# TensorE turns rows in place of DMA transposes, and a search over list schedules orders the attention

## Chip, core and metric

The kernel runs on one core of a Trainium2 chip. The metric is the device time of one execution in microseconds, smaller is better. Engines are named as in the profile: PE is TensorE (PEld its weight loads), DVE is VectorE, ACT is ScalarE, POOL is GpSimd, SP is SyncE, whose only work here is to issue DMAs.

## What is computed

One transformer block with adaptive layer norm, all in float32. `x` is 2 x 2048 rows of 256 features (4096 rows in all).

```
mod = silu(c) @ Wmod                       # six rows of 256 for each of the 2 batches
h   = layernorm(x) * (1 + ca) + sa
x   = x + ga * attention(h)                # 2 heads of 128, one shared k and v, rotary, causal
h   = layernorm(x) * (1 + cb) + sb
gate = softmax(h @ Wg + bg);  thr = sigmoid(h @ Wt + bt) / 8
w    = max(gate - thr, 0), normalised over the 8 experts
x   = x + gb * sum_e w[e] * (gelu(h @ W1[e] + b1[e]) @ W2[e] + b2[e])     # 256 -> 1024 -> 256
```

A row goes only to experts where its weight is above zero, so each expert has a list of rows.

## The kernel before

**Attention stage.** The 4096 rows are 32 tiles of 128. For each tile the function `tile_steps` declares small steps: load `x` (L505), moments (L476 to L483), normalise (`xn`, L516), transpose on PE (`pt`, L525), scale and shift (`hT`, L533/L535), project (`pq`, L548/L553), rotate, scores (`psc`, L600, with a mask matmul L604), exponent (L627), transpose of the probabilities (`ptr`, L673) and their copy out (L677), the product with v (`pav`, L683), the output projection (`po`, L717), residual (L724), second norm (`hx`, L740/L743), the row store to `feats` (L759) and the gate logits (`pl`, L787). For 28 of the 32 tiles the transpose of `hx` that the logits need goes by DMA: POOL splits the float32 words into two planes of 16 bits (`hp`, L750), SP stores them to `feats` and issues a DMA transpose (L771), and POOL or DVE joins the halves (L775). The last four tiles transpose `hx` on PE (`ph`, L767) and ACT copies it out (L782).

**What sets the order.** Every step is put into a `Plan` with an engine, an estimated cost, the steps that it follows, the buffers that it takes and gives back (`room`) and a rank. `Plan.run` plays the steps through once: at each time the ready step of lowest rank goes to a free engine. The order found is the order of the instructions on each engine, for good; on the chip semaphores do the waiting. `first` is the rank of what the start needs, ranks of 999 and above belong to the end.

**Between the stages.** While the attention ends, two items of expert 0 are already worked (`pha`, L1055; `pya`, L1072), their rows gathered and transposed by `fetch`, which also prepares the first item of the expert stage (`xT`). Both halves of a `pya` result share one PSUM tile. `hold` loads the row counts of the experts into registers, all eight in one step on PE.

**Expert stage.** Each expert's list is worked in items of 256 rows (`TI`), the last of an expert in 128 if that is enough. Four loops run side by side, coupled by semaphores:

- PE (`item`, L1266): waits for `ready`, does the first product into PSUM `h` (L1272, 8 chunks `f`, over `HB` = 6 rotating banks), then the second into `y` (L1282).
- ACT: gelu from `h` to `g` (L1307).
- POOL: copies an item's row numbers (`at`, L1441), gathers the rows from `feats` into `xr` (two indirect DMAs, L1397), writes part of the next expert's list (L1413 to L1421, four indirect DMAs, in the first items of an expert), and adds the result of an earlier item to `out` (L1431).
- SP (`turn`, L1231): waits for the gather (`loaded`), transposes `xr` to `xp` by DMA (L1239) and raises `planed`.
- DVE: joins the halves into `xT` (L1335) when the first product of the current item is done, then gates and biases (L1350, L1363, L1374).

POOL may gather into `xr` again when `planed` says that it was read.

Of the kernel before, what the change touches and what calls it, by code (L numbers as in the profile page):

```python
# [15 lines left out]
U16 = mybir.dt.uint16  # L16
# [5 lines left out]
P = 128  # L22
# [19 lines left out]
HB = 6  # L42
# [3 lines left out]
class Plan:  # L46
# [19 lines left out]
    def run(self):  # L66
# [10 lines left out]
        while open_ or ends:  # L77
            for n in sorted(open_, key=lambda n: (self.steps[n][6], n)):
                engs, costs, do, _, take, give, _, late = self.steps[n]
                idle = [(e, c) for e, c in zip(engs, costs) if free.get(e, 0.0) <= now]  # L80
                if not idle or ready[n] > now:
                    continue
                eng, cost = idle[0]
                if any(self.room[r] < take.count(r) for r in take):
                    continue
                for r in take:
                    self.room[r] -= 1
                free[eng] = now + cost
                ends.append((now + cost + late, n))
                open_.discard(n)  # L90
                order.append((n, eng))
            times = [e for e, _ in ends] + [f for f in free.values() if f > now]
            times += [ready[n] for n in open_ if ready[n] > now]
            now = min(t for t in times if t > now)
            for e, n in [x for x in ends if x[0] <= now]:
                ends.remove((e, n))
                for r in self.steps[n][5]:
                    self.room[r] += 1
                for m in then[n]:
                    need[m] -= 1  # L100
                    ready[m] = max(ready[m], e + LINK)
                    if need[m] == 0:
                        open_.add(m)
        assert len(order) == len(self.steps)
# [6 lines left out]
def adaln_block_kernel(ctx, tc, x, wqkvT, woT, wgt, bgt, w1, b1T, w2, b2, cT, wmod, rope, out):  # L111

# [37 lines left out]
    b2_bc = const.tile([P, E, D], F32, name="b2_bc")  # L152
    gb_bc = const.tile([P, B, D], F32, name="gb_bc")
    lists = [dram.tile([NTOK, ENT], F32, name=f"list_{e}") for e in range(E)]
    feats = dram.tile([NTOK, 2 * D], U16, name="feats")
# [11 lines left out]
    with tc.manual_schedule():  # L167
        attention(
            tc, x, wqkvT, woT, wgt, bgt, w1, b1T, w2, b2, cT, wmod, rope, out, ident, counts,
            b1_sb, b2_bc, gb_bc, lists, feats, place, entry, weights, wpool,  # L170
# [6 lines left out]
    for e in range(RES, E):  # L177
# [3 lines left out]
    xr = ep.tile([P, CI * 2 * D], U16, name="xr")  # L181
    xp = ep.tile([P, CI * 2 * KD, P], U16, name="xp")
# [10 lines left out]
    mcur = ep.tile([P, CI, ENT], F32, name="mcur")  # L193
    to = ep.tile([P, NW], I32, name="to")
    new = ep.tile([P, NW, ENT], F32, name="new")
    hs = [pp.tile([P, TI], F32, name=f"h{z}") for z in range(HB)]
    ys = [pp.tile([P, D], F32, name=f"y{c}") for c in range(CI)]
    experts(
        tc, nc, lists, feats, out.rearrange("b t d -> (b t) d"), counts, ident, b1_sb, b2_bc,
        gb_bc, w1, w2, weights, xr, xp, kept, gs, gate, part, yb, yo_end, who_end, sheets, at, mcur, to, new,  # L200
# [4 lines left out]
def attention(  # L205
    tc, x, wqkvT, woT, wgt, bgt, w1, b1T, w2, b2, cT, wmod, rope, out, ident, counts,
    b1_sb, b2_bc, gb_bc, lists, feats, place, entry, weights, wpool,
# [6 lines left out]
    room = {"ps": 6, "pav": 2, "x": 9, "s": 16, "pT": 3, "hx": 4, "hp": 3, "qT": 3, "big": 3, "xn": 3,  # L214
            "hT": 2, "hT2": 2, "hpT": 2, "aT": 2, "g_sb": 1, "sign": 1, "size": 1}
# [86 lines left out]
    def load(dst, src, kb, rank=first, **how):  # L302
        return plan.add(
            "SP", max(0.5, kb / 360.0), lambda: nc.sync.dma_start(dst, src), late=2.0, rank=rank,
            **how
# [8 lines left out]
    plan.add("PE", 3.4, lambda: idle_work(8), take=["ps"], give=["ps"], rank=first - 5)  # L314
# [13 lines left out]
    for t0, t1 in [(0, 1), (1, 4)] + [(q, q + 4) for q in range(4, NT, 4)]:  # L328
# [14 lines left out]
    l_b2 = load(  # L343
        b2_bc.rearrange("p e d -> p (e d)"), b2.rearrange("e d -> (e d)").partition_broadcast(P),
        1024, rank=6.0,
    )
# [27 lines left out]

    def by_feature():
        box["pm"] = pm = ps_tile("pm")
        for j in range(2 * KD):
            for k in range(KD):
                nc.tensor.matmul(
                    pm[:, j * B : (j + 1) * B], wm_0[:, k, ts(j, P)], sc[:, k, :],  # L380
                    start=(k == 0), stop=(k == KD - 1),
                )
# [9 lines left out]
    m_pe = plan.add("PE", 2.0, by_feature, after=[s_sc, l_m0], take=["ps"], rank=first)  # L392
# [95 lines left out]
    def tile_steps(b, i, r, group, g):  # L488
# [14 lines left out]
        def load_x():  # L503
# [6 lines left out]
            "SP", 0.5, load_x, late=2.0, take=["x"], rank=first + early[r] if r in early else r  # L510
# [237 lines left out]
        def halves():  # L748
            st["hp"] = work([P, 2, D], "hp", u, U16)
            nc.gpsimd.tensor_copy(  # L750
                st["hp"], st["hx"].bitcast(U16).rearrange("p (d two) -> p two d", two=2)
            )


        by_dma = r < NTOK // P - 4
        n_f = add("POOL", 0.65, halves, [n_h], take=["hp"], give=["hx"] if by_dma else [])
        n_hp = add(
            "SP", 0.5,
            lambda: nc.sync.dma_start(  # L759
                feats[ts(b * NT + i, P), :], st["hp"].rearrange("p two d -> p (two d)")  # L760
            ), [n_f], late=2.0, give=[] if by_dma else ["hp"],
        )
# [6 lines left out]
        def turn_halves():  # L769
            st["hpT"] = work([P, 2 * KD, P], "hpT", u, U16)  # L770
            nc.sync.dma_start_transpose(st["hpT"], st["hp"].rearrange("p two d -> p (two d)"))  # L771

        def join_halves(eng):
            st["hT2"] = work([P, KD, P], "hT2", u)
            of[eng].tensor_copy(  # L775
                st["hT2"].bitcast(U16).rearrange("p k (t two) -> p k t two", two=2),
                st["hpT"].rearrange("p (two k) t -> p k t two", two=2),
            )

        def hT2_out():  # L780
            st["hT2"] = work([P, KD, P], "hT2", u)
            nc.scalar.copy(st["hT2"].rearrange("p k t -> p (k t)"), st["ph"][:, :D])  # L782
# [14 lines left out]
        if by_dma:  # L797
            n_t = add("SP", 1.3, turn_halves, [n_f, n_hp], late=2.2, take=["hpT"], give=["hp"])
            n_t = add(
                ["POOL", "DVE"], [0.66, 0.58], join_halves, [n_t], take=["hT2"], give=["hpT"]  # L800
            )
        else:
            n_t = add("PE", 0.32, turn_h, [n_h], take=["ps"])
            n_t = add("ACT", 0.38, hT2_out, [n_t, n_f], take=["hT2"], give=["ps", "hx"])
# [171 lines left out]
    def fetch(index, u, after, to, take=(), low=low):  # L976
# [3 lines left out]
        def gather():  # L980
            st["xr"] = work([P, CI * 2 * D], "g_sb", "_r" + u, U16)
            for c in range(CI):
                nc.gpsimd.indirect_dma_start(
                    out=st["xr"][:, ts(c, 2 * D)],
# [5 lines left out]
        def turn():  # L990
            st["xp"] = work([P, CI * 2 * KD, P], "sign", "_p" + u, U16)
            nc.sync.dma_start_transpose(st["xp"], st["xr"])

        def join():
            dst = to().bitcast(U16).rearrange("p k (c t two) -> p c k t two", c=CI, two=2)
            src = st["xp"].rearrange("p (c two k) t -> p c k t two", c=CI, two=2)
            for c in range(CI):
                nc.vector.tensor_copy(dst[:, c], src[:, c])

        n = low("POOL", 2.6, gather, after, late=3.0, take=["g_sb"])  # L1000
        n = low("SP", 0.1, turn, [n], late=3.5, take=["sign"], give=["g_sb"])
        return low("DVE", 0.8, join, [n], take=take, give=["sign"])
# [23 lines left out]
    before_gelu = list(last_exp)  # L1026
    for k in range(AHEAD):
# [40 lines left out]
        def second(c, f0, st=st, k=k):  # L1068
            if (c, f0) == (0, 0):
                st["py"] = ps_tile(f"pya_{k}")  # L1070
            for f in range(f0, f0 + NF // 2):
                nc.tensor.matmul(  # L1072
                    st["py"][:, ts(c, D)], st["g", f // 2 * 2][:, ds(f % 2 * TI + c * P, P)], weights[0][1][:, f, :],
                    start=(f == 0), stop=(f == NF - 1),
                )

        def result(c, k=k, st=st):
            yo = kept.yo[k][:, c, :]
            nc.vector.tensor_tensor(yo, st["py"][:, ts(c, D)], b2_bc[:, 0, :], ALU.add)
# [3 lines left out]
        for f0 in range(0, NF, 2):  # L1083
# [5 lines left out]
            )  # L1089
            n_a.append(low(  # L1090
# [4 lines left out]
        for c in range(CI):  # L1095
            for f0 in (0, NF // 2):
# [3 lines left out]
                    take=["ps"] if (c, f0) == (0, 0) else [],  # L1100
                    give=["s"] * (NF // 2) if (c, f0) == (CI - 1, NF // 2) else [],
                )
            n_r.append(low(
                "DVE", 0.85, lambda c=c, result=result: result(c), [n, n_g, l_b2],
                give=["ps", "size"] if c == CI - 1 else [],
# [29 lines left out]
    def hold(name, eng, columns):  # L1135
        def load():
            kept.count[name] = {at: register(nc, eng, counts, at) for at in columns}
# [4 lines left out]
    low("PE", 2.0, hold("PE", nc.tensor, range(E)), [n_total] + n_ahead)  # L1142
# [20 lines left out]
def experts(  # L1163
    tc, nc, lists, feats, rows, counts, ident, b1_sb, b2_bc, gb_bc, w1, w2, weights, xr, xp, kept,
# [49 lines left out]
    with tc.tile_critical():  # L1214
        names = (
            "read", "loaded", "planed", "ready", "first", "act", "second", "taken", "parted",
            "gated", "copied", "named", "biased", "added", "waited", "paused", "indexed", "staged",
# [4 lines left out]
        with nc.Block() as block:  # L1222

            @block.sync
            def _(sync):
# [7 lines left out]
                def turn(t):  # L1233

                    sync.wait_ge(sem["loaded"], t * (16 * CI))
                    sync.sem_inc(sem["paused"], 1)
                    sync.wait_ge(sem["ready"], t + 1)
                    sync.sem_inc(sem["paused"], 1)
                    sync.dma_start_transpose(xp, xr).then_inc(sem["planed"], 16)  # L1239

                sync.sem_inc(sem["planed"], 16)
                done, t0 = 1, 0
                for e in range(E):
                    many = items_of(sync, count(sync, e))
                    if e == E - 1:
                        run(sync, many, NTOK // TI, lambda i: turn(t0 + i))
                    else:
                        a = count(sync, E + e)
                        run(sync, a, NP, lambda i: turn(t0 + done + i))
                        read(e + 1)  # L1250
                        t1 = sync.snap(
# [328 lines left out]
```

## Time and profile before

| | us |
|---|---|
| median of 3 runs (1622.19 to 1622.57) | 1622.2 |
| the profiled execution: its time | 1622.67 |
| the profiled execution: first to last instruction (the span) | 1620.5 |
| PE busy | 1596.6 |
| POOL busy | 907.2 |
| DVE busy | 665.1 |
| ACT busy | 588.2 |
| first product of the expert stage starts | 464.22 |
| last product of the expert stage starts its stretch | 1606.01 |

The mean granted clock of PE is 0.995. A float32 matmul shows as two records in the profile, a transpose on PE as one. The length of a record is its time from start to end in a pipeline, so records overlap; the time that one costs PE is the distance from its start to the start of the next.

### The profile page before, as it was taken

The page shows a single profiled execution, that of the slowest core. Times are in us where ns is not written, and L with a number is a line of the kernel's source. Part 1 is how long each engine was busy: PE and PEld are TensorE (multiplying, and loading weights), DVE is VectorE, ACT ScalarE, POOL GpSimd, SP SyncE. Part 2 cuts the span into 40 slices and gives each one's busy share as a digit, 9 for nine tenths or more (in the row PEclk, how much of TensorE's full clock was granted, in tenths as well). Part 3 has the DMA queues.
Part 4 walks back from the last instruction along what each step waited for, and adds up shares of the span by engine and source line. Part 5 has one row for each costly group of instructions (what it writes and reads, how often), then busy time and mean ns, then how long its engine had stood idle before and what let it go on. Part 6 is the DMA issues. An engine that isn't in the chain of part 4 may idle for free.

```text
span 1620.5 us, 26414 instructions
## 1 busy us (share of the span) xinstructions
PE 1596.6 (99%) x7916; PEld 1361.7 (84%) x7916; DVE 665.1 (41%) x2141; ACT 588.2 (36%) x1385; POOL 907.2 (56%) x1063
## 2 busy tenths in 40 slices
PE   8999999999999999999999999999999999999997
PEld 6877777777878888888888888888888888888886
DVE  6888767567422332323323222222322232222322
ACT  5576665655522222222222222222222222222322
POOL 5656524222147767757757765664776477534433
PEclk9999999999999999999999999999999999999998
DMA  6511111101033353434345334433533333333333
GB/s 237 155 40 50 40 40 30 30 21 43 20 96 59 67 114 59 67 56 111 57 69 111 59 64 92 78 59 59 110 58 66 60 60 60 62 58 58 62 56 48
DMA packets 181521, 111.10 MB, mean 69 GB/s; under 512 B 126354, under 2 KB 172050, under 8 KB 181332
## 3 DMA queue, kind: packets, MB, share of 16 engines
q0 software_dynamic: 41968, 46.83, 18.0%
q1 hardware_dynamic: 131348, 50.43, 13.6%
q10 hardware_dynamic: 8144, 13.11, 2.4%
q8 instruction: 28, 0.46, 0.1%
q14 instruction: 33, 0.27, 0.1%
HBM read 51.44 MB, written 31.87 MB: 51 GB/s over the span
## 4 chain that ended last, share of the span: by engine, by line
PE 95%; issue 1%; DVE 1%; POOL 1%; ACT 1%; another core or an unknown queue 0%; DMA 0%; SPq 0%; POOLq 0%; DVEq 0%; ACTq 0%
PE h L1272 35%; PE y L1282 34%; PE pav L683 7%; PE psc L600 7%; PE ptr L673 3%; PE pq L548 2%; PE po L717 2%; PE pya L1072 1%; PE pha L1055 1%; PE pq L553 1%; PE pl L787 1%; POOL list L900 0%; PE pt L525 0%; DMA x<-in_x 0%
## 5 line engine op out<-in xcount | busy, mean ns | idle before, releaser
L1307 ACT ACTIVATE g<-h,b_sb 128x256 f32<-128x256 f32 (+1 forms) x688 | 317.5, 465 | 838.5 <-PE h L1272 737.1
L1282 PE MATMUL y<-w,g 128*128 128x256 f32 x2640 | 585.8, 379 | 2.3 <-ACT g L1307 1.9
L1272 PE MATMUL h<-xT,w 128*128 128x256 f32 (+1 forms) x2752 | 584.9, 371 | 0.1
L1272 PEld LDWEIGHTS h<-xT,w 128*128 128x128 f32 x2752 | 506.1, 190 | 66.4 <-DVE xT L1335 0.8
L1282 PEld LDWEIGHTS y<-w,g 128*128 128x128 f32 x2640 | 500.4, 190 | 72.8 <-ACT g L1307 4.2
L1431 POOL DMA_INDIRECT out<-yo,who x172 | 277.0, 1610 | 219.3 <-DVE yo L1374 163.2
L1421 POOL DMA_INDIRECT list<-new,to x216 | 221.7, 1027 | 93.6 <-issue 69.1
L1363 DVE TENSOR_TENSOR yb<-y,b_bc 128x256 f32<-128x256 f32 x165 | 62.7, 420 | 422.7 <-PE y L1282 375.3
L1397 POOL DMA_INDIRECT xr<-feats,at x172 | 171.7, 998 | 100.4 <-POOL at L1441 70.3
L1335 DVE COPY xT<-xp 128x512 uint16<-128x512 uint16 x172 | 68.7, 441 | 315.6 <-PE h L1272 156.6
L600 PE MATMUL psc<-kT,qT 128*128 128x512 f32 (+3 forms) x320 | 144.1, 532 | 0.8 <-DVE thr L853 0.8
L683 PE MATMUL pav<-pT,v 128*128 128x256 f32 x544 | 143.7, 386 | 0.3 <-ACT pT L677 0.3
L683 PEld LDWEIGHTS pav<-pT,v 128*128 128x128 f32 x544 | 96.4, 190 | 38.9 <-issue 21.2
L627 ACT ACTIVATE s<-s,nmx 128x512 f32<-128x512 f32 (+3 forms) x160 | 104.5, 656 | 38.5 <-DVE nmx L618 38.3
L611 DVE TENSOR_SCALAR_CACHE_REDUCE s<-psc 128x512 f32<-128x512 f32 (+3 forms) x160 | 96.8, 608 | 50.8 <-PE psc L600 36.1
L677 ACT COPY pT<-ptr 128x512 f32<-128x512 f32 (+1 forms) x144 | 77.6, 562 | 56.6 <-PE ptr L673 50.2
L900 POOL DMA_INDIRECT list<-entry,place x40 | 41.9, 1048 | 80.9 <-DVE place L897 47.1
L1350 DVE SCALAR_TENSOR_TENSOR gate<-gb_bc,mcur,part 128x256 f32<-128x256 f32 x172 | 77.0, 488 | 3.0
L673 PEld LDWEIGHTS ptr<-ident,s 128*128 128x128 f32 x544 | 64.8, 141 | 15.4 <-issue 5.7
L673 PE MATMUL ptr<-ident,s 128*128 128x128 f32 x544 | 77.1, 273 | 0.0
L1441 POOL COPY at<-sheet 128x2 int32 x85 | 61.7, 725 | 13.3 <-DMA xp<-xr 11.1
L1374 DVE TENSOR_TENSOR yo<-yb,gate 128x512 f32<-128x512 f32 (+1 forms) x85 | 57.2, 673 | 3.9
(171 smaller groups left out, 1076.4 us busy)
## 6 DMA issues: line engine op xcount, KB each, us to landing
w<-in_w ACTq DMA_DIRECT2D x12, 1024.0 KB
x<-in_x SPq DMA_DIRECT2D x32, 128.0 KB, 4.3
w<-in_w SPq DMA_DIRECT2D x4, 1024.0 KB
out<-x SPq DMA_DIRECT2D x32, 128.0 KB, 1.7
feats<-hp SPq DMA_DIRECT2D x32, 128.0 KB, 1.7
list<-new,to POOLq DMA_INDIRECT x216
xr<-feats,at POOLq DMA_INDIRECT x172
out<-yo,who POOLq DMA_INDIRECT x172
```

What stands on the lines that cost most here:

```text
L600: nc.tensor.matmul(ps[:, :w], st["qT"][:, h, :], kT[:, ds(c * SC, w)], start=True, stop=not last)
L611: nc.vector.tensor_scalar(s[:, :w], st["sc", h, c][:, :w], scale, None, ALU.mult, ALU.max, accum_out=st["mx", h][:, c : c + 1],)
L627: nc.scalar.activation(s[:, :w], s[:, :w], AF.Exp, bias=st["nmx", h], accum_out=st["den"][:, h, c : c + 1],)
L673: nc.tensor.transpose(ptr[:, j, h, :], s[:, ds((c0 + j) * P % SC, P)], ident)
L677: nc.scalar.copy(pT[:, :m], st["ptr", c0][:, :m])
L683: nc.tensor.matmul(st["pav"][:, : NH * P], v[:, c0 + j, :], st["pT", c0][:, j].rearrange("p h t -> p (h t)"), start=(c0 + j == 0), stop=(c ...
L1272: last = pe.matmul(hs[f % HB][:, :w], weights[e][0][:, k, ts(f, P)], xT[:, k, :w], start=(k == 0), stop=(k == KD - 1),)
L1282: last = pe.matmul(ys[c], gs[f][:, ts(c, P)], weights[e][1][:, f, :], start=(f == 0), stop=(f == NF - 1),)
L1307: act.activation(gs[f][:, :w], hs[f % HB][:, :w], AF.Gelu_apprx_tanh, bias=b1_sb[:, at : at + 1],).then_inc(sem["act"], 1)
L1397: pool.indirect_dma_start(out=xr[:, ts(c, 2 * D)], out_offset=None, in_=feats, in_offset=bass.IndirectOffsetOnAxis(ap=at[:, c : c + 1], ax ...
L1421: pool.indirect_dma_start(out=lists[e], out_offset=bass.IndirectOffsetOnAxis(ap=to[:, j : j + 1], axis=0), in_=new[:, j, :], in_offset=Non ...
L1431: pool.indirect_dma_start(out=rows, out_offset=bass.IndirectOffsetOnAxis(ap=who[:, c : c + 1], axis=0), in_=yo[:, c, :], in_offset=None, c ...
```

## The change

1. **Expert stage.** `xr` holds float32 rows. PE transposes them itself: after the first product of item t it waits for the gather of item t+1 and does four transposes of 128 x 128 into a PSUM tile `xt`, then goes on with the second product. DVE copies `xt` to `xT` in one instruction. SP keeps only the reads of the lists. `xt` takes a PSUM bank, so `HB` goes from 6 to 5. POOL waits for `turned` where it waited for `planed`.
2. **Attention.** All 32 tiles transpose `hx` on PE; ACT or DVE copies it out. The split, the DMA transpose and the join are gone, and `feats` gets `hx` as it is. The gathers of `fetch` (two items ahead and the next) are transposed on PE too.
3. **The order.** `Plan.run` tries 13 schedules with fixed pseudo-random numbers: one with the ranks as written, and twelve in which each kind of step (told by the line of its function) gets a common shift of up to 0.3, 1.0 or 2.0 ranks, for ranks from 1 to 900. The shortest by its own estimate is emitted. Early loads are estimated to land after 3.5 us in place of 2.0, and `room` for `x` is 12 in place of 9.
4. **Start.** The modulation of the first norm (`by_feature`) is made as two matmuls of 512 columns, an ACT copy and four small transposes in place of eight narrow matmuls; the idle matmuls ahead of it are 12 in place of 8, and 3 more follow.
5. **Ends of the attention.** The two halves of `pya` get a PSUM tile each. The eight PE register loads become eight steps among the last products. Four idle matmuls at the start of the expert stage become three.
6. **b2.** Expert 0's row is loaded early (128 KB broadcast in place of 1024 KB); the other seven are loaded by ACT's queue when expert 1 begins.

```diff
-HB = 6
+HB = 5
+TRIALS = (0.0,) + (0.3, 1.0, 2.0) * 4
...
+    def run(self):
+        draw = random.Random(0)
+        kinds = sorted({s[2].__code__.co_firstlineno for s in self.steps})
+        best = (float("inf"), None)
+        for w in TRIALS:
+            by = {k: draw.uniform(-w, w) for k in kinds}
+            best = min(best, self.trial([
+                by[s[2].__code__.co_firstlineno] if 1.0 <= s[6] < 900.0 else 0.0
+                for s in self.steps
+            ]), key=lambda found: found[0])
+        now, order = best
...
-    plan.add("PE", 3.4, lambda: idle_work(8), take=["ps"], give=["ps"], rank=first - 5)
+    plan.add("PE", 5.0, lambda: idle_work(12), take=["ps"], give=["ps"], rank=first - 5)
...
-        if by_dma:
-            n_t = add("SP", 1.3, turn_halves, [n_f, n_hp], late=2.2, take=["hpT"], give=["hp"])
-            n_t = add(
-                ["POOL", "DVE"], [0.66, 0.58], join_halves, [n_t], take=["hT2"], give=["hpT"]
-            )
-        else:
-            n_t = add("PE", 0.32, turn_h, [n_h], take=["ps"])
-            n_t = add("ACT", 0.38, hT2_out, [n_t, n_f], take=["hT2"], give=["ps", "hx"])
+        n_t = add("PE", 0.24, turn_h, [n_h], take=["ps"])
+        add(
+            "SP", 0.5, lambda: nc.sync.dma_start(
+                feats[ts(b * NT + i, P), :], st["hx"].bitcast(I32)
+            ), [n_t], late=2.0, give=["hx"],
+        )
+        n_t = add(["ACT", "DVE"], [0.38, 0.42], hT2_out, [n_t], take=["hT2"], give=["ps"])
...
-        n = low("SP", 0.1, turn, [n], late=3.5, take=["sign"], give=["g_sb"])
-        return low("DVE", 0.8, join, [n], take=take, give=["sign"])
+        n = low("PE", 0.46, turn, [n], take=["ps"], give=["g_sb"])
+        return low("DVE", 0.7, lambda: nc.vector.tensor_copy(to(), st["xt"]), [n], take=take,
+                   give=["ps"])
...
-    low("PE", 2.0, hold("PE", nc.tensor, range(E)), [n_total] + n_ahead)
+    for e, n in enumerate(products[-E - 1 : -1]):
+        plan.add("PE", 0.05, hold("PE", nc.tensor, [e]), after=[n_total, n], rank=999.0)
...
             @block.tensor
             def _(pe):
+                def turn(t):
+                    pe.wait_ge(sem["loaded"], t * (16 * CI))
+                    for c in range(CI):
+                        for k in range(KD):
+                            last = pe.transpose(xt[:, k, ts(c, P)], xr[:, c, ts(k, P)], ident)
+                    last.then_inc(sem["turned"], 1)
+
                 def item(e, i, t, parts):
...
                         last.then_inc(sem["first"], 1)
+                    turn(t + 1)
                     for f in range(NF):
...
                 def ready(t):
-                    dve.wait_ge(sem["planed"], t * 16 + 16)
-                    dst = xT.bitcast(U16).rearrange(
-                        "p k (c t two) -> p c k t two", c=CI, two=2
-                    )
-                    src = xp.rearrange("p (c two k) t -> p c k t two", c=CI, two=2)
-                    for c in range(CI):
-                        last = dve.tensor_copy(dst[:, c], src[:, c])
-                    last.then_inc(sem["ready"], 1)
+                    dve.wait_ge(sem["turned"], t + 1)
+                    dve.tensor_copy(xT, xt).then_inc(sem["ready"], 1)
```

## Prediction

> **What bounds the kernel now.** I read the page first: shares of busy time, clock, the costliest groups.
>
> ```profile
> PE 1596.6 (99%) x7916; PEld 1361.7 (84%) x7916; DVE 665.1 (41%) x2141; ACT 588.2 (36%) x1385; POOL 907.2 (56%) x1063
> ...
> PEclk9999999999999999999999999999999999999998
> ...
> L1282 PE MATMUL y<-w,g 128*128 128x256 f32 x2640 | 585.8, 379 | 2.3 <-ACT g L1307 1.9
> L1272 PE MATMUL h<-xT,w 128*128 128x256 f32 (+1 forms) x2752 | 584.9, 371 | 0.1
> ```
>
> PE is busy 99% at full clock, and ahead of 5392 expert records it idled 2.4 us. A busy PE could still hide bubbles, so next comes the chain of waits in order of time, where a half item of the expert stage is one piece:
>
> ```profile
> 485.52 6.91 PE y L1282 x32
> 492.43 6.91 PE h L1272 x32
> 499.33 6.91 PE y L1282 x32
> ```
>
> 32 records in 6.91 us are 0.216 each, back to back, item after item: 13.82 us an item, and nothing but PE work in it. The list of waits agrees: DVE waits 120.4 us for the DMA transposes, yet all PE waiting on another engine comes to these few lines:
>
> ```profile
> DVE xT L1335 <- DMA xp<-xr: 120.4, 34, 4.2
> ...
> PE pt L525 <- DVE xn L516: 4.3, 3, 2.2
> ...
> PE y L1282 <- ACT g L1307: 1.9, 2, 1.1
> ```
>
> So the DMA transposes are wholly hidden, and work put on PE lengthens the end one for one, unless it falls into one of PE's holes. These are at the start (first projection at 10.80 us), after 30.07 us, and between the stages.
>
> **The price of one transpose on PE.** The trace has 544 like it (`ptr`, float32, 128 x 128). Columns: start, length, line.
>
> ```profile
> 302.47 1.08 PE L683 MATMUL pav<-pT,v 128*128 128x256 f32 x4
> 303.39 1.04 PE L673 MATMUL ptr<-ident,s 128*128 128x128 f32 x8
> 304.26 1.02 PE L600 MATMUL psc<-kT,qT 128*128 128x512 f32 x2
> ...
> 310.12 0.60 PE L673 MATMUL ptr<-ident,s 128*128 128x128 f32 x4
> 310.55 1.03 PE L717 MATMUL po<-woG,aT 128*128 128x256 f32 x4
> ```
>
> Start to start, eight cost 0.87 us and four cost 0.43: 0.109 each. The four `pav` ahead of the eight took 0.92, where four at 0.216 are 0.86, so a switch can add 0.06. The row of one `ptr` gives a mean of 273 ns, but that is its length in the pipeline. The Trainium skill (TensorE: Matmul & The Clock Gate, Part 4: PE-mode transpose) gives about 275 ns in a kernel, and adds that transposes don't engage the full clock. By that rule the change would cost 412 x 0.275 = 113 us; by the start distances, with the clock at 9 in these slices, 45. I take the distances. The skill also calls the DMA path the slow one (VectorE: DVE Perf Modes, The three transpose paths: 1309 ns against 390, for bf16). SP's 86 issues here have a median of 1.24 us, and a sum by that rule would gain some 0.9 us per transpose; the waits above say that nothing on PE waits for them, so I credit 0.
>
> **The change part by part**, against the profiled execution (time 1622.67, span 1620.5, 2.2 around it, 0.5 above the median).
>
> *Expert turns.* L1272 has 2752 records, 32 an item: 86 items, so 86 turns. Four transposes are 0.437, with both switches up to 0.51; I take 0.47: 86 x 0.47 = +40.4 (37.6 to 43.8). Nothing hides it. Queued behind `turn` on PE is the second product, and behind that everything. The copy to `xT` (two join copies of 0.43 before, one PSUM read now, like the 0.42 of L1363 per 256 columns, so about 0.8) has the 6.9 us of the second product to hide in. `HB` 5 costs nothing: chunk 5 starts 4.3 us into an item, and the gelu that frees its bank ended 1.6 us in (464.22 to 465.86); without that cover each item would pay the difference. In two places, mid-`y`, PE waits for the gelus of a 128-row item; the turn gives ACT 0.47 us there: -0.9.
>
> *The new wait on the gather.* The gather must now land by the end of the first product; before, it had until some 4 us ahead of the item's end, for transpose and join. First item of the stage:
>
> ```profile
> 464.22 7.07 PE L1272 MATMUL h<-xT,w 128*128 128x256 f32 x32
> ...
> 468.56 0.19 POOL L1441 COPY at<-sheet 128x2 int32 x1
> ...
> 469.59 1.02 POOL L1397 DMA_INDIRECT xr<-feats,at  x1 [0.83 <-POOL at L1441]
> ...
> 470.91 0.95 POOL L1397 DMA_INDIRECT xr<-feats,at  x1 [0.30 <-issue]
> ...
> 471.13 7.07 PE L1282 MATMUL y<-w,g 128*128 128x256 f32 x32
> ...
> 473.99 15.44 SPq L1239 DMA_TRANSPOSE xp<-xr  x2
> ```
>
> SP issues at 473.99, so the gather landed about then, 2.8 us after the first product ended at 471.13: PE stands still, +2.8 (0 to 4), with the second product queued behind. Second item: POOL's next gather was taken up by SP at about 488.2 (473.99 + 15.44 - 1.24). The new PE comes to its second turn at 474.0 + 0.5 + 6.9 + 6.9 = 488.3: just in time. From there POOL's period with list writing is 13.5 (`at` at 482.33, 495.82, 509.26), while PE's is 13.82 + 0.47 = 14.29, so the slack grows by 0.8 an item: 0 further. POOL's own wait, `turned`, is raised half an item before it comes round again; its list writes and adds queue behind it, and DVE's `who` waits for the adds.
>
> *Attention transposes.* 28 tiles x 2, and 3 x 4 for the fetched items: 68 x 0.109 = +7.4. The second price (ACT 0.37 or DVE 0.42 per copy) replaces 0.68 on POOL for the join or 0.45 on DVE, and POOL loses 32 splits of 0.68; POOL and SP get lighter, DVE (up to 43 of 50 us busy) and ACT (up to 32 of 50) hardly change. SP has 31 fewer transpose issues and the row store waits for `hx` alone. Behind `turn_h` on PE lie scores and products of other tiles, with ACT's copies waiting on them; the order puts it where `hx` is estimated done, and estimates of the same quality leave PE nearly without waits today: 0.
>
> *Start.* PE was cold until 14.4 us (the clock in windows of 1 us: 0.50 from 8 to 14). More idle work may keep it warm: projections spaced 0.213 at 10.80 and 0.109 later, so up to -1.7. Against it, `modT` gets longer: 0.65 on ACT, 0.4 on PE and two handovers, while the first idle stretch (3.46 for 16 records) grows by half. I take -1 (-3 to +2).
>
> *Order and buffers.* The hole of 2.2 us after 30.07 waits for an `xn` whose chain lies behind the modulation rows on DVE; it may go or move: -1 (-2 to +2). More `x` buffers and the 1024 KB of b2 off the early queue help only there. Elsewhere the middle of the attention has little to give: `thr` at 138 us cost 0.8.
>
> *Between the stages.*
>
> ```profile
> 457.12 1.99 PE L1072 MATMUL pya<-w,s_g 128*128 128x256 f32 x8 [0.52 <-DVE yo L1079]
> 460.56 1.35 PE L312 MATMUL pi<-ident 128*128 128x128 f32 x10 [1.45 <-issue]
> 463.26 1.13 PE L1294 MATMUL y<-ident 128*128 128x128 f32 x8 [1.34 <-issue]
> ```
>
> Eight records from 457.12 end at 458.85. The 1.7 us until 460.56 I read as the eight register loads, moved under queued products now; the 0.52 wait for `yo` goes with the second PSUM tile; one idle matmul less is 0.2. Together -2.4. If a register load finds `counts` not yet written, PE stops and this turns to +2. The b2 load of expert 1 has a whole item to land before DVE needs it: 0.
>
> Sum: 40.4 - 0.9 + 2.8 + 7.4 - 1 - 1 - 2.4 = +45.3, that is 1668.0 for the profiled execution and **1667.5** for a median.
>
> **The rivals.**
>
> *Faster: the new order pays for the turns.* PE's needed work in the attention, from counts and start distances: `pav` 544 x 0.216 = 117.5; `psc` 224 x 0.43 + 32 x (0.323 + 0.216 + 0.109) = 117.0; masks 64 x 0.06 = 3.8; transposes 616 x 0.109 = 67.1; `pq` 512 x 0.109 = 55.8; `po`, `pya`, `pha` 256 x 0.216 = 55.3; `pl` 128 x 0.09 = 11.5; modulation 5.3. Sum 433. The stage ends at 464.2, so a perfect order gains 31 at most. For this to win, the 412 transposes must cost less than (31 - 2.8) / 412 = 0.068 each. The one 128-column record near that is the bf16 mask, at 0.06; at its price, and with a perfect order, the end is -31 + 2.8 + 24.7, about -3.5: 1619. The float32 `ptr` rows speak against it, and the start can't be ordered away. 4%.
>
> *Slower by more: the gather becomes the bound.* If POOL's period comes above 14.3, PE waits in every item with list writing: 54 of them. At 1 us each, +54 on top: near 1720; half of that, 1695. The 13.5 speaks against it. 6%.
>
> *The transposes at 0.275:* 1622 + 113, about 1735. 2%.
>
> *The order doesn't hold on the chip.* Shortest by estimate isn't shortest on the chip; moved ranks may put PE steps ahead of late DVE work, as with `thr` at 138 us. Ten to twenty such stops of 0.8: +8 to +16, near 1680. 8%. If the search keeps the unmoved ranks, the change does less than it says, and my sum stands.
>
> **How the numbers follow.** The main case has 80%: its turns (37.6 to 43.8), first wait (0 to 4) and the three uncertain credits give 1656 to 1678. The range goes from 1655 to 1682, to take in most of the bad order. About 0.2%, 3 us, is what a measurement can tell from no change. Faster by more than that 3%, within it 1%, slower 96%.
>
> **What would show it.** Start to start, four transposes at 0.44 to 0.51 between each `h` and `y`; an item of 14.3 us; PE waiting some 3 us for `xr` in the first item and not later; first expert product at 464 + 7.4 - 4.4, about 467; PE busy up by some 47 us. Wrong if the expert stage grows by less than 35 or more than 50, or if its start moves by over 10 us either way.

## The result, and the profile after

| | before | changed |
|---|---|---|
| median of 4 runs (us) | 1622.2 | 1666.63 |
| ratio, with its 95% interval | | 1.0279 (1.0261 to 1.0297) |
| profiled execution: time (us) | 1622.67 | 1668.39 |
| profiled execution: span (us) | 1620.5 | 1666.5 |
| first product of the expert stage starts (us) | 464.22 | 465.58 |
| expert stage, from there to the end of the span (us) | 1156.3 | 1200.9 |

The change makes the kernel 2.8% slower, as forecast (1667.5). All but 1.4 us of the 46 us in the span are in the expert stage. The profiled execution is the longest of the four; the ledger below is that of its trace.

The page of the changed kernel, its shares, clock, chain by line and three groups:

```profile
PE 1644.4 (99%) x8332; PEld 1402.0 (84%) x8332; DVE 648.0 (39%) x2048; ACT 591.9 (36%) x1399; POOL 873.1 (52%) x1022
...
PEclk9999999999999999999999999999999999999999
...
PE y L1274 33%; PE h L1263 32%; PE pav L713 7%; PE psc L630 7%; PE ptr L703 3%; PE pq L578 3%; PE xt L1252 2%; PE po L747 2%; DMA xr<-feats,at 1%; PE pya L1076 1%; PE pq L583 1%; PE pha L1059 1%; PE pl L795 1%; PE pi L331 0%; PE pt L555 0%
...
L1274 PE MATMUL y<-w,g 128*128 128x256 f32 x2640 | 587.8, 380 | 0.4
L1263 PE MATMUL h<-xT,w 128*128 128x256 f32 (+1 forms) x2752 | 584.9, 371 | 0.0
...
L1328 DVE COPY xT<-xt 128x512 f32<-128x512 f32 x86 | 59.5, 692 | 345.8 <-PE xt L1252 316.2
```

PE is as full as before, with 48 us more of busy time, at full clock. The two products cost what they did. DVE and POOL have less to do, which nobody was waiting for. New in the chain is `xt`, 2%, and with it a DMA, the gather. PE's instructions in order of time show where `xt` went (start, length):

```profile
484.12 7.07 PE L1263 MATMUL h<-xT,w 128*128 128x256 f32 x32
491.03 0.60 PE L1252 MATMUL xt<-ident,xr 128*128 128x128 f32 x4
491.47 7.07 PE L1274 MATMUL y<-w,g 128*128 128x256 f32 x32
498.38 7.07 PE L1263 MATMUL h<-xT,w 128*128 128x256 f32 x32
```

The four transposes take 0.44 us from start to start, without any loss at the switches, and an item takes 14.26 us where it took 13.82: the turn is simply inserted. That is 86 x 0.44 = 37.8 us. The rest are waits. From the list of what PE waited for (us in total, times, longest):

```profile
PE xt L1252 <- DMA xr<-feats,at: 4.6, 4, 2.5
PE y L1287 <- issue: 1.8, 1, 1.8
...
PE xt L1252 <- issue: 1.2, 1, 1.2
```

The list counts PE's idle time only; from start to start the loss is some 0.2 us larger each time, since the last record runs on past its slot (a product is 7.07 long and 6.91 from start to start). The first item:

```profile
465.58 7.17 PE L1263 MATMUL h<-xT,w 128*128 128x256 f32 x32
475.21 1.11 PE L1252 MATMUL xt<-ident,xr 128*128 128x128 f32 x4 [2.46 <-DMA xr<-feats,at]
476.12 8.17 PE L1274 MATMUL y<-w,g 128*128 128x256 f32 x32
484.12 7.07 PE L1263 MATMUL h<-xT,w 128*128 128x256 f32 x32
```

The first product should be over 6.91 us after 465.58; the turn starts 2.7 us later than that. Then the turn takes 0.91 in place of 0.44 and the second product 8.00 in place of 6.91. The windows of 1 us show why; the column ahead of the last two is the granted clock:

```profile
473.00:474.00 1.00, 0.00 (x0) 0.00 (x0) 0.00 (x0) 0.26 (x1) 0.16 (x1) 1.00 0.81 194
474.00:475.00 1.00, 0.00 (x0) 0.00 (x0) 0.00 (x0) 0.00 (x0) 0.34 (x2) 0.96 0.34 107
475.00:476.00 1.00, 0.79 (x4) 0.79 (x5) 0.00 (x0) 0.00 (x0) 0.22 (x1) 0.50 0.00 0
...
478.00:479.00 1.00, 1.00 (x6) 0.83 (x5) 0.00 (x0) 0.00 (x0) 0.69 (x2) 0.83 0.03 2
```

The clock fell to 0.50 at the end of the wait, for some 3.4 us, and cost 1.6 us more. Four more waits, each at the first whole item of an expert after one of 128 rows, cost 1.10, 0.81, 1.40 and 0.79 from start to start. The third is the longest:

```profile
880.69 7.07 PE L1263 MATMUL h<-xT,w 128*128 128x256 f32 x32
889.00 0.66 PE L1252 MATMUL xt<-ident,xr 128*128 128x128 f32 x4 [1.23 <-issue]
```

The profile names no releaser for this one; it stands at the same place as the other three, with the gather issued and a weight load on the DMA engines (share 1.01 from 880.5 to 887), so I count it with them.

So the expert stage: turns 37.8, first wait 2.7 and cold clock 1.6, later gather waits 4.1, stops of PE in and behind the 128-row items 3.1 where they were 4.3, and 0.4 of small losses in other items of the kernel before that are gone: 44.6 worked out, 44.6 measured.

In the attention, the first projections before (two lines), then the start and the end of the stage in the changed kernel:

```profile
10.80 2.76 PE L548 MATMUL pq<-hT,wqk_sb 128*128 128x128 f32 x12
...
14.21 1.68 PE L548 MATMUL pq<-hT,wqk_sb 128*128 128x128 f32 x12
...
11.47 1.72 PE L578 MATMUL pq<-hT,wqk_sb 128*128 128x128 f32 x12
13.03 0.61 PE L583 MATMUL pq<-wv_sb,hT 128*128 128x128 f32 x4
13.48 1.50 PE L578 MATMUL pq<-hT,wqk_sb 128*128 128x128 f32 x12
...
461.59 1.28 PE L331 MATMUL pi<-ident 128*128 128x128 f32 x10
464.69 0.91 PE L1287 MATMUL y<-ident 128*128 128x128 f32 x6 [1.82 <-issue]
465.58 7.17 PE L1263 MATMUL h<-xT,w 128*128 128x256 f32 x32
```

The first projection starts 0.7 us later than before but runs warm (granted clock 1.00, where it was 0.50 from 8 to 14 us): it takes 2.01 us with its v part where it took 3.41, and the hole after 30 us is gone. From the last `pya` to the first expert product there are 4.0 us where there were 5.4: the gap ahead of the idle matmuls is gone, but the one behind them grew from 1.6 to 2.0.

### The profile page after: what moved, and what is told of

It reads as the page before. It is cut to its first block, busy times and chain, and to the rows that moved or that the text cites. A ratio compares the mean times of both kernels' runs of the same rounds, so it can differ in the third digit from the quotient of the medians.

```text
span 1666.5 us, 26347 instructions
## 1 busy us (share of the span) xinstructions
PE 1644.4 (99%) x8332; PEld 1402.0 (84%) x8332; DVE 648.0 (39%) x2048; ACT 591.9 (36%) x1399; POOL 873.1 (52%) x1022
## 4 chain that ended last, share of the span: by engine, by line
PE 94%; POOL 2%; issue 2%; DMA 1%; DVE 0%; POOLq 0%; ACT 0%; another core or an unknown queue 0%; DVEq 0%; SPq 0%; ACTq 0%
PE y L1274 33%; PE h L1263 32%; PE pav L713 7%; PE psc L630 7%; PE ptr L703 3%; PE pq L578 3%; PE xt L1252 2%; PE po L747 2%; DMA xr<-feats,at 1%; PE pya L1076 1%; PE pq L583 1%; PE pha L1059 1%; PE pl L795 1%; PE pi L331 0%; PE pt L555 0%
## 5 line engine op out<-in xcount | busy, mean ns | idle before, releaser
L1274 PEld LDWEIGHTS y<-w,g 128*128 128x128 f32 x2640 | 494.9, 190 | 68.0 <-ACT g L1300 4.4
L1357 DVE TENSOR_TENSOR yb<-y,b_rest 128x256 f32<-128x256 f32 x148 | 56.2, 420 | 441.9 <-PE y L1274 410.8
L1328 DVE COPY xT<-xt 128x512 f32<-128x512 f32 x86 | 59.5, 692 | 345.8 <-PE xt L1252 316.2
L1439 POOL COPY at<-sheet 128x2 int32 x85 | 31.8, 375 | 62.8 <-PE xt L1252 61.1
L512 POOL TENSOR_SCALAR rstdf<-mvf 128x1 f32<-128x1 f32 x32 | 8.8, 276 | 99.0 <-DVE mvf L508 79.0
```

Source lines behind the costliest of these rows:

```text
L1274: last = pe.matmul(ys[c], gs[f][:, ts(c, P)], weights[e][1][:, f, :], start=(f == 0), stop=(f == NF - 1),)
```

## The experiments

The kernel before was timed beside each group of kernels. Its median was 1618.7 to 1619.9 in three groups and 1622.3 in the fourth, so ratios and kernels of one group are what to compare.

**Which part pays, and which gains.** Four kernels in one group; before 1618.76.

*expert_dma*: the changed kernel, with DMA transposes, issued by SP, in the expert stage and the fetches, and with POOL's split and the 16-bit row store of before. The main lines:

```diff
-HB = 5
+HB = 6
...
+        by_dma = False
...
+                    sync.dma_start_transpose(xp, xr).then_inc(sem["planed"], 16)
...
-                    turn(t + 1)
```

> The changed kernel with the expert stage, the fetches and the 16-bit row store of before (DMA transposes, HB 6); the attention keeps its 32 transposes on PE, the search, the new start and ends. Theory A (every PE transpose costs its start distance of 0.109 us, and the expert turns plus their waits on the gather are nearly the whole loss): first expert product at 464 to 466 us, expert stage back at about 1156 us, time about 1623. Rival B (the reordered attention carries a good part of the loss, or disturbs the expert stage): over 1635.

Measured: 1619.14, ratio 0.9998 (0.9989 to 1.0006). First expert product at 463.98, expert stage 1153.0. The loss is gone, though all 32 tiles of the attention still transpose on PE. Rival B falls. In this trace the clock stood at 0.50 from 463.75 to 467.2 us, so the first expert product took 8.49 us in place of 6.91; the expert stage holds that 1.6 too.

*order_only*: as expert_dma, with `by_dma` as before the change.

```diff
-        by_dma = False
+        by_dma = r < NTOK // P - 4
```

> The kernel before with DMA transposes everywhere, plus the search over 13 schedules, the new start, the new ends and the late b2. Theory A: what the change gained, without what it paid; the changed kernel's attention ended 1.4 us later although it held 68 x 0.109 = 7.4 us more PE work, so some 6 us were gained: 1616, faster than before. Rival B (the gain in the attention came from the transposes leaving the DMA path, through POOL and SP getting lighter): 1621 to 1624, no gain left.

Measured: 1613.76, ratio 0.9964 (0.995 to 0.9977). This beats both kernels, and rival B, which left no gain, falls. Its end of the attention:

```profile
455.43 1.28 PE L332 MATMUL pi<-ident 128*128 128x128 f32 x10
458.70 0.91 PE L1330 MATMUL y<-ident 128*128 128x128 f32 x6 [1.99 <-issue]
459.44 7.08 PE L1308 MATMUL h<-xT,w 128*128 128x256 f32 x32
```

The first expert product starts at 459.44, 4.5 us ahead of expert_dma, and the median is 5.4 us lower. The 56 transposes of `hx` that differ are worth 56 x 0.109 = 6.1 by their start distances. So those, too, are paid for the most part, as far as two kernels with an order each can tell; the 1.6 of cold clock behind expert_dma's first product start is not theirs. The gains of the change are the 5.0 us by which this kernel beats the one before.

*ends_only*: as order_only, with the ranks as written.

```diff
-TRIALS = (0.0,) + (0.3, 1.0, 2.0) * 4
+TRIALS = (0.0,)
```

> As order_only, but only the schedule with the ranks as written. Theory A (the gain is the warm start and the gap between the stages): within 2 us of order_only, about 1617. Rival C (the search brings the gain): 1621 or more.

Measured: 1615.04, ratio 0.9973 (0.9962 to 0.9985), first expert product at 460.62. Of the 5.0 us gained, 3.7 are there without the search, and rival C falls here. The intervals of the two ratios overlap, since both hold the scatter of the kernel before (1617.6 to 1621.67). Yet every execution with the search (1612.86 to 1614.0) is below every one without (1614.05 to 1616.22), and its first expert product is 1.2 earlier, so about that much is the search's here.

*plain_order*: the changed kernel with the same edit of `TRIALS`.

> The changed kernel with only the schedule with the ranks as written. Theory A: within 3 us of the changed kernel, 1666 to 1669. Rival C (the moved ranks are worth much, either way): over 1672, or below 1662.

Measured: 1661.85, ratio 1.0264 (1.025 to 1.0278). By the letter that is rival C (below 1662), but the expected figures were those of the first group, where the kernel before stood 3.4 higher. Against expert_dma's 1619.14 it is 42.7 more, for PE turns in the expert stage and the fetches: the traces give 37.8 to the turns, 5.0 to the first and the later gather waits (2.70, 1.58, 0.71) and 1.25 to a later first expert product, less the 1.6 that expert_dma lost to its clock. To compare the search itself, both orders ran side by side in a later group (before 1618.68).

> The changed kernel, to stand beside plain_order_2 on one chip. Theory A: ratio to before 1.026 to 1.028.

> The changed kernel with the unmoved ranks, beside after_3 on one chip. Theory A (the middle of the attention has nothing to give, so the search is worth 2 us at most either way): within 2 us of after_3. Rival C (the search is worth more): 3 us or more above, or below, it.

Measured: 1661.15, ratio 1.0259 (1.0245 to 1.0274), and 1662.46, ratio 1.0268 (1.0254 to 1.0283). Again 1.3 us, again with overlapping intervals, and again every execution with the search (1660.88 to 1661.25) is below every one without (1661.28 to 1663.31). But only 0.3 of it lies ahead of the first expert product (465.26 and 465.58 us), the rest in the expert stage. Rival C falls: the search is worth a gain of some 1 us in one pair and less in the other.

**What a turn costs.** *turn_twice* (before 1619.87):

```diff
-                    for c in range(CI):
+                    for c in [*range(CI), *range(CI)]:
                         for k in range(KD):
                             last = pe.transpose(xt[:, k, ts(c, P)], xr[:, c, ts(k, P)], ident)
```

> The changed kernel with each of an item's four transposes done twice into the same place. Theory A (transposes cost PE their start distance, nothing hides them): 86 x 0.437 = 37.6 more, 1704, an item of 14.69 us. Rival E (the loss is the waits; the transposes fill bubbles): less than 15 more. Rival F (0.273 each, the length of their records): 94 more, 1760.

Measured: 1696.97, ratio 1.0482 (1.0466 to 1.0498). Two items in its middle:

```profile
511.32 7.07 PE L1263 MATMUL h<-xT,w 128*128 128x256 f32 x32
518.22 1.04 PE L1252 MATMUL xt<-ident,xr 128*128 128x128 f32 x8
519.10 7.07 PE L1274 MATMUL y<-w,g 128*128 128x256 f32 x32
```

Eight transposes take 0.88, the item 14.69: 0.44 more, exactly as much again. The median is 7 below the 1704 expected. In this group the stops in 128-row items were absent (3.1 in the changed kernel's trace), the later gather waits came to 1.06 in place of 4.1, and the clock fell earlier, during the first product (0.50 from 465.1 to 468.5 us). There it cost nothing of its own, because PE had to wait for the gather anyway: 2.56 us were lost ahead of the first turn, of which only 0.6 was idle. Rivals E and F fall: nothing hides a turn, and the length of a record is not its cost.

**The waits on the gather.** *turn_mid* moves the turn behind half of the second product:

```diff
-                    turn(t + 1)
                     for f in range(NF):
...
+                        if f == NF // 2:
+                            turn(t + 1)
```

> The changed kernel with the turn moved behind half of the second product, 3.5 us later in an item, so that the gather has longer to land. Theory A (the loss is 86 turns of 0.44 us, about 38, plus waits on the gather at the start of the stage and at the ends of experts, about 7 with the cold clock that follows the first): the waits go, the turns stay, time 1659 to 1662. Rival D (the late gather only shifts: POOL is the bound there, and the wait comes back as a wait on xT): unchanged, 1666.

Measured: 1656.22, ratio 1.0226 (1.0212 to 1.024). Against turn_twice of the same group it is 40.8 lower: 37.8 of second turns, and waits of 2.56 and 1.06. This is below what both theories expected, again in a group without the stops. Its list of waits has no gather in it; it begins:

```profile
PE y L1288 <- issue: 1.8, 1, 1.8
PE pi L331 <- POOL ident masks.py:199: 1.4, 1, 1.4
PE pt L555 <- DVE xn L546: 0.7, 1, 0.7
```

To set it against the changed kernel on one chip, both were run again with a third (before 1622.34).

> The changed kernel itself, beside turn_mid and no_weight_loads on one chip. Theory A: expert stage as on the first chip within the waits on the gather, 1660 to 1666, with turns of 0.44 us in every item.

> The same kernel as turn_mid, now beside the changed kernel on the same chip. Theory A: 4 to 9 us below after_again, by as much as PE waits on the gather there, and no such wait left. Rival D (the wait only moves): equal.

Measured: 1667.9, ratio 1.0279 (1.0264 to 1.0293), and 1665.52, ratio 1.0259 (1.0241 to 1.0277). The changed kernel is 1.9 above what was expected of it. The gain of turn_mid is 2.4 with overlapping intervals, less than theory A said. The waits on the gather are gone again, but here another came:

```profile
PE h L1263 <- DVE xT L1329: 6.5, 4, 2.1
```

In this group ACT and DVE stood still for 1 to 3 us in the 128-row items, in every kernel (DVE sat idle 5.44 us ahead of one `xT` copy, and the profile names no engine of this core as what it waited for). Turning later leaves only 1.7 us of second product to hide the copy in a 128-row item, so the stop reaches PE. After one of them, at 1338 us, the clock also fell to 0.50, another 1.8. Where the stops were absent, in the group of turn_twice, turn_mid showed no such wait; the changed kernel was not run there, but turn_mid's ratio of 1.0226 lies below the 1.0259 of after_3, another group without the stops. So rival D is near the truth for this group in its time, though not in its reason: what came back is the stops of ACT and DVE, not a late POOL.

*no_weight_loads* leaves out ACT's loads of `w1` and `w2` in the expert stage:

```diff
-                                hs[f % HB][:, :w], weights[e][0][:, k, ts(f, P)], xT[:, k, :w],
+                                hs[f % HB][:, :w], weights[e % RES][0][:, k, ts(f, P)], xT[:, k, :w],
...
-                    if e + RES < E:
+                    if False:
```

> The changed kernel without the loads of the weights of experts 2 to 7 during the expert stage; those experts work with the weights of experts 0 and 1, so the work on PE is the same and the values are not. Theory G (PE waits on the gather at the start of the stage and at the first item of an expert because 2 MB of weights, issued at that moment, share the DMA engines with it): the waits at the experts' first items go, the first shrinks to 1 us or less, 3 to 5 us below after_again. Rival H (POOL issues the gather too late there, whatever the DMA engines do): the waits stay, within 1 us of after_again.

Measured: 1663.03, ratio 1.0249 (1.0235 to 1.0263), 4.9 below after_again. In the two traces the later gather waits went from 3.5 to none and the stops in 128-row items from 5.0 to 5.9; these executions are 2.9 apart, and where the rest of the 4.9 lies no trace shows. First the changed kernel at the first item of expert 1, POOL and PE, and the window (DMA share and GB/s last):

```profile
590.54 1.02 POOL L1395 DMA_INDIRECT xr<-feats,at  x1 [1.35 <-issue]
591.87 1.20 POOL L1395 DMA_INDIRECT xr<-feats,at  x1 [0.30 <-issue]
...
590.08 7.07 PE L1263 MATMUL h<-xT,w 128*128 128x256 f32 x32
598.43 0.66 PE L1252 MATMUL xt<-ident,xr 128*128 128x128 f32 x4 [1.28 <-DMA xr<-feats,at]
...
592.00:597.00 5.00, 5.00 (x24) 4.18 (x22) 2.01 (x6) 2.85 (x6) 3.57 (x6) 1.00 0.98 371
```

Then the kernel without the loads:

```profile
590.43 1.02 POOL L1390 DMA_INDIRECT xr<-feats,at  x1 [1.35 <-issue]
591.76 0.99 POOL L1390 DMA_INDIRECT xr<-feats,at  x1 [0.30 <-issue]
...
590.29 7.07 PE L1259 MATMUL h<-xT,w 128*128 128x256 f32 x32
597.19 0.60 PE L1248 MATMUL xt<-ident,xr 128*128 128x128 f32 x4
...
592.00:597.00 5.00, 5.00 (x25) 4.39 (x24) 1.34 (x4) 2.84 (x6) 3.56 (x6) 1.00 0.37 108
```

POOL issued at the same moment in both. With the loads the DMA engines are at 0.98 and the rows come too late; without them the turn follows the product at once. That is theory G, for the experts' first items. The changed kernel's own trace agrees: experts 6 and 7 load no weights, also begin after an item of 128 rows, and show no wait. The short item seems to be needed too, though one case is all there is: expert 4 loads weights but begins after a whole item, and shows none. From one turn to the next PE takes 14.26 us, but 0.44 + 3.45 + 6.91 = 10.8 when the item between is of 128 rows, so the gather has less time.

The very first wait, however, is still there (2.52 from start to start, 2.3 of it idle), where theory G wanted 1 at most: for that one rival H is right. POOL first adds two results of the items worked ahead and writes one list entry, and only then gathers:

```profile
464.53 1.63 POOL L1456 DMA_INDIRECT out<-yo,front  x1 [10.82 <-issue]
...
468.41 0.99 POOL L1467 DMA_INDIRECT list<-entry,place  x1 [0.30 <-issue]
...
470.45 1.01 POOL L1390 DMA_INDIRECT xr<-feats,at  x1 [0.85 <-POOL at L1434]
...
474.55 0.66 PE L1248 MATMUL xt<-ident,xr 128*128 128x128 f32 x4 [2.27 <-DMA xr<-feats,at]
```

The second of its two gathers was issued by 472.7, when the first product was already over (465.12 + 6.91 = 472.0).

*before_again* is one more execution of the kernel before in that group.

> One look at the kernel before on this chip, for the waits of the second product on ACT at the ends of experts. Theory A: first expert product at 463 to 465, an item of 13.81.

Measured: 1623.48, first expert product at 464.11, an item of 13.81, and the same stops at 128-row items (2.24 and 1.89 in two of them, where PE waits for ACT's gelu).

## Why the prediction was right, step by step

- *The price of a transpose* (0.109, from start to start) held: the turn is 0.44, where four make 0.437. I had added 0.03 a turn for switches; there are none, so the term of 40.4 was 37.8. An item is longer by the turn alone, so `HB` 5 and the copy to `xT` cost nothing, as forecast. The Trainium skill's figure of about 275 ns (TensorE: Matmul & The Clock Gate, Part 4: PE-mode transpose) fits the length of one record here, a median of 273 ns for `xt`, but not the cost: four took 0.44 us at a clock of 1.00.
- *The DMA transposes were hidden*: taking them out of the expert stage gained nothing, as putting them back showed (expert_dma, ratio 0.9998).
- *The new wait, first item*: +2.8 forecast, 2.7 measured. The cold clock behind it, 1.6, was not in the sum. It is not the same in every execution (see the last section).
- *"0 further"* was wrong: 4.1 in four later waits. The step that failed looked at POOL's period in steady items. Where an item of 128 rows ends an expert, the next turn comes sooner, and 2 MB of weights are on the DMA engines just then. The earlier deadline was seen; that neither the deadline nor the landing time is a constant was not.
- *ACT's waits in 128-row items*: -0.9 forecast, -1.2 measured over all such stops. But between before_again and after_again the same stops went only from 5.1 to 5.0, so the agreement is luck.
- *Attention*: +7.4 - 4.4 = +3.0 forecast, +1.4 measured. The transposes are confirmed for the most part (4.5 for 56, 6.1 by my price). For the gains, an estimate: count the records that PE needs, without idle matmuls, at their steady start distances. By 40 us the kernel before had done 26.5 us of them and the changed one 29.0, so the credits for start and order were 2.5 where I took 2. Between 40 and 454 us it gained another 1.5, where I had said that the middle has little to give (the wait of 0.8 for `thr`, for one, is gone). From there to the first expert product it gained 2.1 where I took 2.4: the wait for `yo` and the gap ahead of the idle matmuls went as forecast, the gap behind them grew by 0.4.
- The errors of the sum were -2.6 (turns), -0.1 and +1.6 (first wait, clock), +4.1 (later waits), -0.3 (stops), -1.6 (attention) and -0.4 (small losses): +0.7 together. That the median was met to 1 us is partly their cancelling, and so partly luck.
- *The rivals*: the search and the other gains outside the transposes are 5 us (order_only), far from the 31 that a perfect order could have brought; the gather is late in some items and not in all.

## What to carry to other kernels

Before moving work to an engine, ask whether it is the one that is full: here work that was free on the DMA engines and SP cost 38 us on PE, at exactly the start distance of the same instruction elsewhere in the trace. A consumer that is moved earlier also moves a deadline, so look for the items where the deadline is tightest, and at what else is on the DMA engines then, not only at the steady period. A change of several parts can be split: the part that gained (order, start, ends) is worth keeping without the part that paid, and gives 0.9964 (0.995 to 0.9977).

## What the hardware showed

- After short stops of PE the granted clock fell to 0.50 for about 3.4 us in some executions and not in others. Between the stages PE stood idle for 1.8 to 2.0 us: the clock fell behind it in expert_dma, after_again, plain_order and turn_twice, and not in eight other traces of the new kernels (seven with 1.8 to 2.0, no_weight_loads with 1.5). At the first gather wait it fell after 2.46 us idle in the changed kernel, and not after 2.17 to 2.39 in after_3, plain_order_2 and no_weight_loads. What tells them apart was not tried.
- Where the clock fell ahead of the gather wait, the wait hid it; behind the wait it cost 1.6 us. In after_again the first product is slow, and PE then idles 0.53 us in place of 2.46 (start of the stage, and the clock in the column ahead of the last two):

```profile
465.03 8.86 PE L1263 MATMUL h<-xT,w 128*128 128x256 f32 x32
474.41 0.66 PE L1252 MATMUL xt<-ident,xr 128*128 128x128 f32 x4 [0.53 <-DMA xr<-feats,at]
...
466.00:467.00 1.00, 1.00 (x4) 0.74 (x3) 0.45 (x2) 0.15 (x1) 0.75 (x1) 0.50 1.04 430
```

- In two of the five sets of runs ACT and DVE stood still for 1 to 3 us in the 128-row items, which run once per expert, in the kernel before too; in the other sets they did not. The trace shows no releaser for these stops, or one that had long been done. The kernel before was some 2.3 to 3.7 us slower in those two sets. The cause stays open; the page counts DMA of instructions too (0.46 MB on queue q8 in the kernel before), and whether that has a part in it was not tried.
- A gather of 2 x 128 rows was taken up 1.8 us after its second issue ended in no_weight_loads, with no weights on the DMA engines (472.71 to 474.55), and 5.4 us after it in after_again with a weight load beside it, 371 GB/s in all (591.87 + 1.20 to 598.43).
